# Six convolutions moved from GpSimd to TensorE, and the first sequence's helpers moved earlier, in a fused two-layer block

## Chip, cores and metric

The kernel runs on one core of a Trainium2 chip. Everything is one launch. The metric is the device time of that launch in microseconds (us); lower is better. The kernel before took 853.75 us in the median of three runs (847.93 to 856.35).

A core has five engines that each work through a list of instructions in order: TensorE (PE in the profile; its weight loads are listed apart as PEld), VectorE (DVE), ScalarE (ACT), GpSimd (POOL) and SyncE (SP), which here only issues transfers. An instruction that waits holds up all that stand behind it on its engine.

## What is computed

Two layers on an input of 4 sequences, 256 steps and 512 features, in float32. Layer 0 is attention plus a gated feed-forward; the change doesn't touch it. Layer 1 is a selective scan (Mamba) plus a small mixture of experts. This is the scan's part, shortened:

```python
proj = hidden_states @ in_proj_w                 # 512 -> 2 * 1024
x, z = jnp.split(proj, 2, axis=-1)               # each (4, 256, 1024), then transposed
xc = conv_b[None, :, None]
for k in range(4):                               # causal convolution along time, per channel
    xc = xc + conv_w[None, :, k:k + 1] * xp[:, :, k:k + Lq]
xc = jax.nn.silu(xc)
ssm_p = jnp.einsum('bdl,ed->ble', xc, x_proj_w)  # -> dt_r (32), Bm (16), Cm (16), each normalised
dt = jax.nn.softplus(jnp.einsum('blr,dr->bdl', dt_r, dt_proj_w) + dt_bias[None, :, None])
# per channel and state n = 0..15:  h_t = exp(dt_t * A_n) * h_(t-1) + dt_t * Bm_t * x_t ;  y_t = sum_n Cm_t * h_t
y = (ys + D_param[None, :, None] * xc) * jax.nn.silu(z)
return jnp.einsum('bdl,hd->blh', y, out_proj_w)
```

## The kernel before

**Tiling.** The 1024 channels of layer 1 are 8 chunks of 128 (`DC`), and two chunks are a pair, so that a sequence has four pairs. The 16 states are four groups (`NU`). One scan handles one chunk and one group for all 256 steps: 128 rows by 4 x 256 values. A sequence is 32 scans (`PER`), the four sequences are 128. Below, "scan u" is scan u of the sequence named, counted from 0, and "pair (b, p)" is pair p of sequence b.

**One scan's chain.** `decays` (ACT, L958, four instructions) makes exp(dt A). `scan_in` (DVE, L964) makes bx in PSUM from two spread inputs: `brow` and `dus`. `scan` (DVE, L979) runs the recurrence into tile `h`, and GpSimd multiplies it by C into tile `hc` (L984). `states_sum` (PE, L996) sums `hc` into the PSUM tile `ysum`, of which there is one. After a chunk's four scans `close_chunk` (DVE, L1000) multiplies `ysum` by the silu of z, `sz`; the next chunk's first sum (L994) waits for that.

**Order.** It is written out by hand. The main loop runs over the scans; for scan u it records, in this order: `decays(u + 2)`; the side work listed for u with `put`; `scan_in(u)`; a `close_chunk` if scan u - 2 was the last of its chunk; `scan(u)`; the side work listed with `put_late`; and `states_sum(u - 1)`. Each engine gets its instructions in that order.

**The side work that the change touches.**

- *Convolution* of the next sequence, two chunks at a time. `px_mm` (PE, L753) fills the PSUM tile `px`. `conv_in` (ACT) copies it into a padded tile (L762), makes four diagonal matrices `dg` for the first chunk (L767), and for the second chunk writes one product with the bias (L768) and three products `tap` (L772). `conv_taps` multiplies the four diagonals with shifted views of the padded tile on PE (L789, four matmuls), lets ACT add the bias (L791), and adds the second chunk's three taps on GpSimd (L795). Sequence 0's own convolution, before the loop, is done otherwise and stays.
- *Step widths* of the second half of sequence 0: `step_in` (PE and ACT, scans 5 and 6), `step_exp` (ACT, scan 7), `step_out` (three GpSimd additions L892, L894, L896 for each of two quarters q, the last followed by a store `dtd` to DRAM), `step_x` (GpSimd product L903 and store `dud`), and `spread`, which reads a chunk back into `dts` or `dus` with four transfers. All these transfers stand in one list on SP, together with the loads of weights `w_in`, `bw`, `lb` and `ow`.
- *The end of layer 0.* The last matmuls `po` of layer 0 (`down`, L469) run beside scans 0 to 2. Their memory becomes the pool `act` (`open_act`), which holds most tiles `h`, `hc` and two of three `decay` tiles. Because that memory is taken until then, scans 0 to 3 use lent tiles: the table `lent` names, per scan, a tag of another tile that is free for a while (`w_in`, `u`, `e`, `lw`). `step_in` writes the next tile with the tag `u`, `step_exp` those with `e` and `lw`. A new tile under a tag waits for the last reader of the old one.
- `add_last` (DVE, L481) adds the last row blocks of layer 0 after scans 1, 3 and 4; the one after scan 4 needs the very last `po`.

The order before, for the lines that the change edits:

```python
for q, us in enumerate(((5, 6, 7), (10, 12, 14)) if b else ((8, 9, 11), (15, 17, 18))):
    for k in range(3):
        put(b, us[k], step_out, b, 1, q, k)
for p, u in ((2, 8 if b else 13), (3, 16 if b else 19)):
    put(b, u, step_x, b, p)
for c in range(2, DC):
    o = 0 if b or c < 4 else 2
    put(b, 3 if c == 2 and not b else 4 * c - 6 + o, spread, "dt", b, c)
    put(b, 4 * c - 4 + o, spread, "du", b, c)
```

The pairs of sequence b + 1 are convolved beside sequence b: `conv_in` of pair p at scan 9 + 2p of sequence 0 and 8 + 2p of the others, `conv_taps` one scan later.

Of the kernel before, what the change touches and what calls it, by code (L numbers as in the profile page):

```python
# [8 lines left out]
F32 = mybir.dt.float32  # L9

F32R = mybir.dt.float32r
AF = mybir.ActivationFunctionType
ALU = mybir.AluOpType
# [4 lines left out]
P = 128  # L18
B, S, D = 4, 256, 512
# [6 lines left out]
DIN, NST, KC, RK = 1024, 16, 4, 32  # L26
# [11 lines left out]
V_CW, V_CB, V_DB, V_AL, V_D, V_END = 0, 4, 5, 6, 22, 23  # L38
# [3 lines left out]
def block_kernel(  # L42
# [24 lines left out]
    nc = tc.nc  # L67
    mm = nc.tensor.matmul
# [50 lines left out]
    live = {}  # L119
# [530 lines left out]
    NU = NST // NG  # L650
# [97 lines left out]
    def px_mm(b, p, i):  # L748
# [3 lines left out]
        for hc in range(HC):  # L752
            mm(px[:, i, :], lhsT=w[:, i, hc, :], rhs=xns[b][:, hc, :],  # L753
               start=(hc == 0), stop=(hc == HC - 1))

    def conv_in(b, p):


        px = live["px", b, p]
        if p == 0:  # L760
            xcs[b] = (act if b % 3 else w1).tile([P, DC, S], F32, tag=f"xc{b % 3}", name="xc")
        nc.scalar.copy(pads[p % 2][:, :, KC - 1 :], px)  # L762
        v = [vec[:, 2 * p + i, :] for i in range(2)]
        if b:
            dg = live["dg"] = w1.tile([P, KC, P], F32, tag="dg", name="dg")
            for k in range(KC):
                nc.scalar.activation(dg[:, k, :], ident, AF.Identity, scale=v[0][:, V_CW + k : V_CW + k + 1])  # L767
        nc.scalar.activation(xcs[b][:, 2 * p + 1, :], px[:, 1, :], AF.Identity,  # L768
                             bias=v[1][:, V_CB : V_CB + 1], scale=v[1][:, V_CW + KC - 1 : V_CW + KC])
        tp = w1.tile([P, KC - 1, S], F32, tag="tap", name="tap")  # L770
        for k in range(KC - 1):
            nc.scalar.activation(tp[:, k, :], pads[p % 2][:, 1, k : k + S], AF.Identity,  # L772
                                 scale=v[1][:, V_CW + k : V_CW + k + 1])
        live["tap"] = tp
        if b == 0:
            nc.scalar.activation(px[:, 0, :], px[:, 0, :], AF.Identity, bias=v[0][:, V_CB : V_CB + 1],
                                 scale=v[0][:, V_CW + KC - 1 : V_CW + KC])

    def conv_taps(b, p):
        px, c = live["px", b, p], 2 * p  # L780
        if b == 0:
            for k in range(KC - 1):
                nc.vector.scalar_tensor_tensor(
                    px[:, 0, :] if k < KC - 2 else xcs[b][:, c, :], pads[p % 2][:, 0, k : k + S],
                    vec[:, c, V_CW + k : V_CW + k + 1], px[:, 0, :], ALU.mult, ALU.add,
                )
        else:
            for k in range(KC):
                mm(px[:, 0, :], lhsT=live["dg"][:, k, :], rhs=pads[p % 2][:, 0, k : k + S],  # L789
                   start=(k == 0), stop=(k == KC - 1))  # L790
            nc.scalar.activation(xcs[b][:, c, :], px[:, 0, :], AF.Identity,  # L791
                                 bias=vec[:, c, V_CB : V_CB + 1])
        xc = xcs[b][:, c + 1, :]
        for k in range(KC - 1):
            nc.gpsimd.tensor_tensor(xc, xc, live["tap"][:, k, :], ALU.add)  # L795

    def conv_silu(b, z=None):
        nc.scalar.activation(xcs[b], xcs[b], AF.Silu)
# [130 lines left out]
    def gate_silu(b, *ps):  # L929
# [5 lines left out]


    lent = {
        "d": ("d", "w_in", "d", "w_in"), "h": ("w_in", "u", "e", "u"),
        "hc": ("w_in", "lw", "w_in", "lw"),
    }  # L940

    def lend(n, u):
# [56 lines left out]
    def close_chunk(b, c):  # L999
        nc.vector.tensor_tensor(  # L1000
            xcs[b][:, c, :], ysum, szs[b, c // 2][:, c % 2, :], ALU.mult
        )
# [216 lines left out]
    for b in range(B):  # L1219
# [36 lines left out]
        put(b, 2 if b else 6, step_in, b, 1, 1)  # L1256
        put(b, 3 if b else 7, step_exp, b, 1)

        for q, us in enumerate(((5, 6, 7), (10, 12, 14)) if b else ((8, 9, 11), (15, 17, 18))):
            for k in range(3):  # L1260
                put(b, us[k], step_out, b, 1, q, k)
        for p, u in ((2, 8 if b else 13), (3, 16 if b else 19)):
            put(b, u, step_x, b, p)
        for c in range(2, DC):
            o = 0 if b or c < 4 else 2
            put(b, 3 if c == 2 and not b else 4 * c - 6 + o, spread, "dt", b, c)
            put(b, 4 * c - 4 + o, spread, "du", b, c)
        put(b, 10, load_z, b, 2)
# [64 lines left out]
    for u in range(total + 2):  # L1333
        if 3 <= u < total - 2:
            decays(u + 2)
        for f, a in at.get(u, ()):
            f(*a)
        if u < total:
            if u:
                scan_in(u)  # L1340
        last = u - 2
        if last >= 0 and last % NU == NU - 1:
            c = last % PER // NU
            close_chunk(last // PER, c)
            if last // PER == B - 1:
                late.append(c)
        if u < total:
            scan(u, 1 if u < total - 1 else 4)
            if u < 3:
                decays(u + 2)  # L1350
        for f, a in late_at.get(u, ()):
            f(*a)
        if late and u >= total - PER + 22:
            c = late.pop(0)
            for i in range(2):
                out_mm(B - 1, i, c)
        if 1 <= u <= total:
            states_sum(u - 1)
        if u < 3:
            go(ff, (9, 12, 100)[u])  # L1360
        if u == 2:
            open_act()
# [105 lines left out]
```

## Time and profile before

The profile is of one execution, which took 852.26 us; its span on the core is 850.5 us, so 1.8 us lie around it. The median of the three runs is 853.75 us.

| engine | busy us | share of the span | what it does most |
|---|---|---|---|
| TensorE | 740.6 | 87% | matmuls of both layers |
| VectorE | 669.6 | 79% | scans L979 (288.0), inputs L964 (157.7) |
| ScalarE | 538.6 | 63% | decays L958 (213.3) |
| GpSimd | 489.1 | 58% | products L984 (301.6), taps L795 (32.8) |

The first scan's input starts at 333 us and the last scan ends at about 839 us, so the scan loop is 506 us of the span. Durations that recur below: a scan input takes 1.23 us and a scan 2.29 us, and where VectorE waits for nothing two scans are 3.69 us apart; the product on GpSimd takes 2.36 us; three taps on GpSimd take 2.34 us; the four matmuls of a diagonal convolution take 2.00 us, with the next work starting 1.84 us after their start. In time lines a row is: start in us, duration in us, engine, line, operation, output and inputs with their shapes, how many were merged, and in brackets the idle time of the engine just before it with what ended it. PEclk is the TensorE clock that was granted, as a share of the full one.

### The profile page before, as it was taken

To read this page: it belongs to the slowest core of one execution; us is meant where nothing else is said; L and a number is where in the kernel's file an instruction comes from. 1 tells how busy PE (TensorE), PEld (TensorE's weight loads), DVE (VectorE), ACT (ScalarE), POOL (GpSimd) and SP (SyncE) were. 2 spreads that over 40 slices of the span, in tenths; PEclk is the share of its full clock that TensorE was granted. 3 is DMA by queue.
4 is the path that set the end of the run, shared out by engine and by line. 5 is a ranking of instruction groups with operands and counts; after the bars stand their busy time and mean duration, and the time that the engine had idled before them with its cause. 6 is when DMAs were issued, how large, how long until landed. Compare 5 with 4: busy or idle time off the path is not lost.

```text
span 850.5 us, 10982 instructions
## 1 busy us (share of the span) xinstructions
PE 740.6 (87%) x3798; PEld 423.6 (50%) x3798; DVE 669.6 (79%) x647; ACT 538.6 (63%) x1061; POOL 489.1 (58%) x376
## 2 busy tenths in 40 slices
PE   5999999989999899989778888887898997956875
PEld 3565546656555676656444346344356444312331
DVE  4597755478744435798799999899999999999996
ACT  4225565223566267599885789786888885855561
POOL 3223322001343333669967689869599759697664
PEclk9999999899999999999898999989999979998998
DMA  7234332001222322555751644433553343443400
GB/s 223 68 94 125 88 86 62 0 1 38 75 75 79 113 56 63 139 147 161 206 142 50 173 137 124 123 100 109 156 155 99 102 112 102 109 119 105 112 25 25
DMA packets 67202, 86.71 MB, mean 102 GB/s; under 512 B 12061, under 2 KB 52009, under 8 KB 66762
## 3 DMA queue, kind: packets, MB, share of 16 engines
q1 hardware_dynamic: 57786, 67.12, 28.5%
q0 software_dynamic: 9072, 18.35, 7.8%
q8 instruction: 30, 0.49, 0.2%
q10 hardware_dynamic: 288, 0.52, 0.2%
q14 instruction: 26, 0.21, 0.1%
HBM read 66.58 MB, written 10.22 MB: 90 GB/s over the span
## 4 chain that ended last, share of the span: by engine, by line
PE 37%; DVE 30%; POOL 12%; ACT 8%; issue 6%; DMA 4%; SPq 1%; DVEq 0%; POOLq 0%; ACTq 0%
DVE h L979 18%; POOL hc L984 7%; PE pu L444 6%; PE pg L444 6%; DVE bx L964 6%; ACT decay L958 4%; PE av L397 4%; PE po L469 3%; PE scT L386 2%; DVE mpl L354 2%; PE px L753 2%; POOL xc L795 2%; PE pz L926 2%; DMA dus<-dud 2%; PE ysum L996 1%
## 5 line engine op out<-in xcount | busy, mean ns | idle before, releaser
L984 POOL TENSOR_TENSOR hc<-h,cr 128x1024 f32<-128x1024 f32 (+1 forms) x130 | 301.6, 2322 | 96.4 <-DVE h L979 76.6
L979 DVE TENSOR_TENSOR_SCAN h<-decay,bx 128x1024 f32<-128x1024 f32 (+1 forms) x129 | 288.0, 2234 | 16.3 <-PE po L469 4.0
L958 ACT ACTIVATE decay<-dts,aneg 128x255 f32<-128x255 f32 x504 | 213.3, 498 | 97.5 <-DVE h L979 87.2
L964 DVE TENSOR_TENSOR bx<-brow,dus 128x1024 f32<-128x1024 f32 x128 | 157.7, 1232 | 8.7 <-DMA dus<-dud 4.6
L996 PE MATMUL ysum<-hc,stack 128*32 128x256 f32 x1024 | 88.1, 413 | 60.1 <-POOL hc L984 59.8
L456 POOL TENSOR_TENSOR hlo<-g,hhi 128x512 fp32r<-128x512 f32 x28 | 35.9, 1281 | 118.3 <-ACT hhi L455 118.3
L427 POOL DMA_DIRECT2D wgu<-in_wgu x56 | 31.2, 558 | 97.3 <-PE pg L444 95.9
L354 DVE TENSOR_REDUCE mpl<-sc 128x4 f32<-128x1024 f32 x64 | 76.4, 1217 | 12.4 <-PE sc L352 12.2
L996 PEld LDWEIGHTS ysum<-hc,stack 128*32 128x32 f32 x1024 | 21.2, 111 | 120.7 <-POOL hc L984 98.1
L388 ACT ACTIVATE pe<-scT 128x1024 f32<-128x1024 f32 x64 | 64.0, 1023 | 23.4 <-PE sc L352 16.8
L1088 PE MATMUL po<-ow,xc 128*128 128x512 f32 x128 | 70.4, 659 | 2.2 <-DVE xc L1000 2.2
L926 PE MATMUL pz<-xn1T,w_in 128*128 128x256 f32 x256 | 67.5, 411 | 0.0
L753 PE MATMUL px<-xn1T,w_in 128*128 128x256 f32 x256 | 61.8, 387 | 0.1
L926 PEld LDWEIGHTS pz<-xn1T,w_in 128*128 128x128 f32 x256 | 49.0, 200 | 19.0 <-issue 10.8
L753 PEld LDWEIGHTS px<-xn1T,w_in 128*128 128x128 f32 x256 | 48.2, 192 | 13.1 <-issue 4.3
L452 DVE SCALAR_TENSOR_TENSOR g<-g,pg 128x512 f32<-128x512 f32 x28 | 19.2, 686 | 41.5 <-ACT g L451 41.5
L444 PE MATMUL pu<-xhi,wgu 128*128 128x512 f32 x112 | 48.7, 435 | 2.3 <-DMA wgu<-in_wgu 2.3
L469 PE MATMUL po<-wd,hhi 128*128 128x512 f32 x112 | 50.3, 449 | 0.0
L444 PE MATMUL pg<-xhi,wgu 128*128 128x512 f32 x112 | 48.9, 437 | 0.0
L455 ACT CAST hhi<-g 128x512 fp32r<-128x512 f32 x28 | 17.3, 619 | 48.5 <-DVE g L454 48.5
L444 PE MATMUL pu<-xlo,wgu 128*128 128x512 f32 x112 | 45.4, 405 | 0.0
L469 PE MATMUL po<-wd,hlo 128*128 128x512 f32 x112 | 45.0, 401 | 0.0
(230 smaller groups left out, 1251.7 us busy)
## 6 DMA issues: line engine op xcount, KB each, us to landing
dts<-dtd SPq DMA_DIRECT2D x124, 128.0 KB, 2.9
dus<-dud SPq DMA_DIRECT2D x124, 128.0 KB, 3.0
wgu<-in_wgu POOLq DMA_DIRECT2D x56, 256.0 KB, 2.8
w_in<-in_inx SPq DMA_DIRECT2D x16, 512.0 KB, 4.3
w_in<-in_inz SPq DMA_DIRECT2D x16, 512.0 KB, 4.9
dtd<-dt SPq DMA_DIRECT2D x15, 256.0 KB, 2.2
dud<-du SPq DMA_DIRECT2D x15, 256.0 KB, 2.2
wd<-in_wd POOLq DMA_DIRECT2D x7, 512.0 KB, 3.6
```

The costliest lines, as they stand in the source:

```text
L354: nc.vector.tensor_reduce(mpl2[b % 2][:, qb, 2 * hp : 2 * hp + 2, 16 + 2 * gq : 18 + 2 * gq], sc.rearrange("p i (f k) -> p i f k", f=2), A ...
L388: nc.scalar.activation(pes[b, k][:, 2 * t : 2 * t + 2, :], sc, AF.Exp)
L444: mm(ps, lhsT=wgus[i][:, hc, :], rhs=xs[j][:, hc, :], start=(hc == 0 and j == 0), stop=(hc == HC - 1 and j == 1))
L469: mm(po, lhsT=hids[th][j][:, m, i * P : (i + 1) * P], rhs=wd[:, m, :], start=False, stop=(m == MC - 1 and j == 1))
L753: mm(px[:, i, :], lhsT=w[:, i, hc, :], rhs=xns[b][:, hc, :], start=(hc == 0), stop=(hc == HC - 1))
L926: mm(pz[:, i, :], lhsT=w[:, i, hc, :], rhs=xns[b][:, hc, :], start=(hc == 0), stop=(hc == HC - 1))
L958: nc.scalar.activation(da[:, k, 1:], live["dts", b, c][:, k, 1:], AF.Exp, scale=aneg[:, c, k, g : g + 1])
L964: nc.vector.tensor_tensor(bx, brow[g // 2][:, g % 2, :].unsqueeze(1).to_broadcast([P, NG, S]), live["dus", b, c], ALU.mult)
L979: nc.vector.tensor_tensor_scan(h[:, n].rearrange("p n t -> p (n t)"), da[:, n].rearrange("p n t -> p (n t)"), bx[:, n].rearrange("p n t -> ...
L984: (nc.vector if k == NG - 1 else nc.gpsimd).tensor_tensor(hc[:, n], h[:, n], crows[b][:, g, :].unsqueeze(1).to_broadcast([P, NG // parts, ...
L996: mm(ysum[k * NB : (k + 1) * NB, :], lhsT=stack, rhs=hc[:, k, :], start=False, stop=(g == NU - 1))
L1088: mm(live["po", b, i], lhsT=xcs[b][:, c, i * P : (i + 1) * P], rhs=late_w["ow"][:, c, :], start=False, stop=(c == DC - 1))
```

## The change

Three things change; all lie in layer 1's loop.

1. For six pairs, (1, 0), (1, 3), (2, 1), (2, 3), (3, 1) and (3, 3), the second chunk is convolved as the first is: ACT makes four more diagonals in the memory of `tap`, PE multiplies them into the second half of `px`, and ACT adds the bias. The three GpSimd additions, the biased product L768 and the three taps L772 go, for these pairs.
2. In sequence 0 `step_out`, `step_x` and the spreads of chunks 4 to 7 stand one or two scans earlier.
3. Scan 4 of sequence 0 gets lent tiles too (`h` in `e`, `hc` in `u`), and the first `close_chunk` moves from before scan 5 to behind it.

```diff
+    both = ((1, 0), (1, 3), (2, 1), (2, 3), (3, 1), (3, 3))
+
     def conv_in(b, p):
...
-        nc.scalar.activation(xcs[b][:, 2 * p + 1, :], px[:, 1, :], AF.Identity,
-                             bias=v[1][:, V_CB : V_CB + 1], scale=v[1][:, V_CW + KC - 1 : V_CW + KC])
-        tp = w1.tile([P, KC - 1, S], F32, tag="tap", name="tap")
-        for k in range(KC - 1):
-            nc.scalar.activation(tp[:, k, :], pads[p % 2][:, 1, k : k + S], AF.Identity,
-                                 scale=v[1][:, V_CW + k : V_CW + k + 1])
-        live["tap"] = tp
+        tp = live["tap"] = w1.tile([P, KC - 1, S], F32, tag="tap", name="tap")
+        if (b, p) in both:
+            tp = tp.rearrange("p k t -> p (k t)")
+            for k in range(KC):
+                nc.scalar.activation(tp[:, k * P : (k + 1) * P], ident, AF.Identity,
+                                     scale=v[1][:, V_CW + k : V_CW + k + 1])
+        else:
...
     def conv_taps(b, p):
...
         xc = xcs[b][:, c + 1, :]
-        for k in range(KC - 1):
-            nc.gpsimd.tensor_tensor(xc, xc, live["tap"][:, k, :], ALU.add)
+        if (b, p) in both:
+            dg = live["tap"].rearrange("p k t -> p (k t)")
+            for k in range(KC):
+                mm(px[:, 1, :], lhsT=dg[:, k * P : (k + 1) * P], rhs=pads[p % 2][:, 1, k : k + S],
+                   start=(k == 0), stop=(k == KC - 1))
+            nc.scalar.activation(xc, px[:, 1, :], AF.Identity, bias=vec[:, c + 1, V_CB : V_CB + 1])
+        else:
+            for k in range(KC - 1):
+                nc.gpsimd.tensor_tensor(xc, xc, live["tap"][:, k, :], ALU.add)
...
     lent = {
-        "d": ("d", "w_in", "d", "w_in"), "h": ("w_in", "u", "e", "u"),
-        "hc": ("w_in", "lw", "w_in", "lw"),
+        "d": ("d", "w_in", "d", "w_in"), "h": ("w_in", "u", "e", "u", "e"),
+        "hc": ("w_in", "lw", "w_in", "lw", "u"),
     }
...
-        for q, us in enumerate(((5, 6, 7), (10, 12, 14)) if b else ((8, 9, 11), (15, 17, 18))):
+        for q, us in enumerate(((5, 6, 7), (10, 12, 14)) if b else ((8, 9, 10), (13, 15, 16))):
...
-        for p, u in ((2, 8 if b else 13), (3, 16 if b else 19)):
+        for p, u in ((2, 8 if b else 11), (3, 16 if b else 17)):
             put(b, u, step_x, b, p)
         for c in range(2, DC):
-            o = 0 if b or c < 4 else 2
+            o = 0 if b or c < 4 else 1
...
-            close_chunk(last // PER, c)
+            if c or last > NU:
+                close_chunk(last // PER, c)
...
             scan(u, 1 if u < total - 1 else 4)
+            if last == NU - 1:
+
+                close_chunk(0, 0)
```

On the engines this gives: PE has four more matmuls (and ACT one more biased copy) right behind the diagonal convolution of each of the six pairs; GpSimd lacks 18 additions; on SP the store `dtd` of chunks 4 and 5 comes before the loads `w_in` and `bw`, the store `dud` before a spread and the loads `w_in` and `lb`, and the later stores and spreads of sequence 0 follow one or two places earlier.

## The prediction

> **What bounds the kernel now.** The page first: TensorE is busiest, yet the chain that ended last is shared.
>
> ```profile
> PE 740.6 (87%) x3798; PEld 423.6 (50%) x3798; DVE 669.6 (79%) x647; ACT 538.6 (63%) x1061; POOL 489.1 (58%) x376
> PE 37%; DVE 30%; POOL 12%; ACT 8%; issue 6%; DMA 4%; SPq 1%; DVEq 0%; POOLq 0%; ACTq 0%
> ```
>
> Layer 0 gives TensorE's share; the scan loop, 333 to 839 us, is the stage to read. So next VectorE's instructions in order of time, keeping those with idle time in front. These are all of 0.3 us or more up to the last scan:
>
> ```profile
> 355.55 2.29 DVE L979 TENSOR_TENSOR_SCAN h<-decay,bx 128x1024 f32<-128x1024 f32 x1 [3.96 <-PE po L469]
> 360.74 0.43 DVE L1000 TENSOR_TENSOR xc<-ysum,sz 128x256 f32<-128x256 f32 x1 [1.18 <-ACT sz L932]
> 376.83 0.42 DVE L1000 TENSOR_TENSOR xc<-ysum,sz 128x256 f32<-128x256 f32 x1 [1.17 <-PE ysum L996]
> 394.64 0.43 DVE L1000 TENSOR_TENSOR xc<-ysum,sz 128x256 f32<-128x256 f32 x1 [2.87 <-PE ysum L996]
> 407.78 1.23 DVE L964 TENSOR_TENSOR bx<-brow,dus 128x1024 f32<-128x1024 f32 x1 [3.18 <-DMA dus<-dud]
> 424.03 1.23 DVE L964 TENSOR_TENSOR bx<-brow,dus 128x1024 f32<-128x1024 f32 x1 [1.43 <-DMA dus<-dud]
> 541.28 0.42 DVE L1000 TENSOR_TENSOR xc<-ysum,sz 128x256 f32<-128x256 f32 x1 [1.82 <-PE ysum L996]
> 571.84 0.42 DVE L1000 TENSOR_TENSOR xc<-ysum,sz 128x256 f32<-128x256 f32 x1 [0.53 <-PE ysum L996]
> 664.02 0.42 DVE L1000 TENSOR_TENSOR xc<-ysum,sz 128x256 f32<-128x256 f32 x1 [1.39 <-PE ysum L996]
> ```
>
> They sum to 17.5 us, 13.8 of it in sequence 0. That is all a change to helpers can win here: the loop is VectorE's, 3.69 us a scan, and the question is only what becomes of these waits. Sequence 0 needs the other engines' lists. ACT, then PE:
>
> ```profile
> 365.04 0.45 ACT L853 ACTIVATE u<-pdt,vec 128x256 f32<-128x256 f32 x1
> 382.86 1.70 ACT L958 ACTIVATE decay<-dts,aneg 128x255 f32<-128x255 f32 x4
> 384.69 0.47 ACT L791 ACTIVATE xc<-px,vec 128x256 f32<-128x256 f32 x1
> 365.64 0.66 PE L996 MATMUL ysum<-hc,stack 128*32 128x256 f32 x8
> 366.63 1.13 PE L848 MATMUL pdt<-nrm,dtw 32*128 32x256 f32 x4 [0.32 <-ACT dt L854]
> 381.81 2.84 PE L789 MATMUL px<-pad,dg 128*128 128x256 f32 x8 [2.05 <-ACT xc L768]
> 384.45 2.77 PE L753 MATMUL px<-xn1T,w_in 128*128 128x256 f32 x8
> 390.21 2.00 PE L789 MATMUL px<-pad,dg 128*128 128x256 f32 x8
> ```
>
> ACT is busy without a gap from 355.50 to 384.56, and again from 387.26 to 409.8; PE idles only 0.32, 2.05 and 0.33 us from 365 to 410. So there VectorE has slack, and PE and ACT have none. One more view, stretches with the granted clock (third number from the right):
>
> ```profile
> 381.80:384.50 2.70, 2.69 (x9) 2.21 (x10) 2.56 (x2) 2.70 (x7) 2.54 (x4) 0.69 0.00 0
> 387.20:390.00 2.80, 2.80 (x25) 1.70 (x24) 2.67 (x2) 2.74 (x8) 2.80 (x3) 1.00 0.52 127
> ```
>
> After 2.05 us of idle PE ran at 0.69 for 5.4 us.
>
> **Scan 4 in lent tiles.** Its decay is ready at 347.8 and its input bx at 351.6, so it runs 351.6 to 353.9 instead of from 355.55. But `add_last` behind it needs the last `po`, 355.5. Then 0.66 for it, 1.23 for bx 5, and scan 5 at 357.4 (its decay, ACT from 355.50, is ready at 357.15). `close_chunk` still has to await `sz`, 360.11 + 0.60. It ends at 361.1, and scan 6 starts at 362.4, not 364.73: 2.3 us early.
>
> **What the lent `u` costs.** `step_in` of scan 5 writes the next `u`, so its first ACT instruction (365.04) now waits for the sums of scan 4, recorded after it on PE: 365.64 + 0.66, so 366.37, 1.33 later. PE can't be earlier: its transposes before wait for ACT's xnt (1.92 us idle to 362.89), and xnt follows `sz`. Queued behind on ACT are the rest of `step_in`, two copies, the decays of scan 8 and `step_exp`; on PE pdt L848 waits for the buffer that ACT empties, 366.63 becoming 367.96, and from there PE runs back to back to the sums of scan 7. So the second `close_chunk` moves from 376.83 to 378.16. At scan 9 the 2.3 us early are 1.3 us late. (At nothing, if PE were ahead; a wait can't gain.)
>
> **Pair (1, 0), two groups on PE.** ACT: four diagonals (1.18 us) and a second biased copy (0.40) replace the product (0.45) and the taps (1.20): equal. PE: 1.84 us more. The built order adds a turn: the second group writes the same `px` tile and waits for ACT's copy L791 of the first, and ACT has the decays of scan 12 ahead of that copy. With the shift of 1.33 the copy runs 385.4 to 385.85. The first group may start with its first diagonal, 381.8, and ends at 383.7, so PE stands 2.2 us. No row shows this turn; bounds from the rows: 0.5 us (ACT's 0.47 copy alone) and 2.2. I take 2.2, since ACT's list here has no gap. Then the second group and px L753 take either 1.84 + 1.83 (390.21 to 392.05 and on, full clock) or 2.64 + 2.70 (381.81 to 387.15). The sums of scan 9 so start at 389.6 or 391.2, against 387.15: 2.45 or 4.05 late. The nearest row, 2.05 us idle, had the slow clock, and so had 1.92 and 2.24: I take 4.05. The Trainium skill, "TensorE: Matmul & The Clock Gate", Part 1, says the clock halves after at least one idle window of some 3.4 us; the trace disagrees (0.69 after 2.05), and with the rule the full-clock end of my sum would hold.
>
> PE and ACT carry this on without a gap: the copy for pair (1, 1) waits for px. The third `close_chunk` comes at 397.1 or 398.6, not 394.64.
>
> **Step widths earlier.** GpSimd loses the taps of (1, 0); L896 follows the product of scan 9 and ends near 385.2 instead of 388.45. `dtd` goes out before `w_in` and `bw` instead of behind them, where it took 6.66 us. `dud` now stands behind both (the `w_in` waits for px, 389.6 to 391.2), so give it those 6.7 us: landed by 399, spread by 404. VectorE wants it 9.66 us after scan 13 begins (394.98 to 404.64 before), that is 407.1 or 408.6. The 3.18 us go, but scan 16 starts at most 0.7 earlier or 0.8 later: the lateness of PE has eaten them. The first spread of chunk 5 comes behind `dud` of the next quarter on SP, that is behind L903 of scan 17, ending at 416.5 or so; landed by 422, when VectorE asks at 425 or later. So 1.43 us go.
>
> **Pair (1, 3).** Again 1.84 us and a turn, now behind the decays of scan 18. The sums of scan 15, ended at 410.0 before, end at 415.1 (full) or 417.5 (slow). The fourth `close_chunk`, at 412.61 before, waits for them: 2.5 or 5.0 late. Less 1.43, sequence 0 costs 1.1 or 3.6 us.
>
> **Sequences 1 and 2.** GpSimd was last there: from 497 to 540 it has no gap, and taps of 2.3 us sit ahead of its products.
>
> ```profile
> 535.44 2.33 POOL L795 TENSOR_TENSOR xc<-xc,tap 128x256 f32<-128x256 f32 x3
> 537.73 2.35 POOL L984 TENSOR_TENSOR hc<-h,cr 128x1024 f32<-128x1024 f32 x1
> ```
>
> Without them the product of scan 15 ends at 536.9, not 540.1. PE takes its place: group one of (2, 1) 516.21 to 518.05, turn 0.7, group two to 520.6, then px, sums (0.57), px, and the sums of scan 11 start at 524.85, not 523.80: a new wait of 1.0 at `close_chunk`. On the same list px L753, L994, sums, pz (1.84), sums, pz, two groups with a turn of 0.5, sums, out (1.0), sums: `close_chunk` at 540.95, not 541.28. So -0.3. In sequence 2 the router's 1.05 us (pr L1011) stand on that list too: 123.15 us later that gives 665.15 against 664.02, +1.1. The turns are short there because ACT has gaps; PE has none over 0.8 us, so the clock stays up.
>
> **Sum.** 852.26 (span 850.5 plus 1.8 around it) + 3.6 - 0.3 + 1.1 = 856.7. With full clock 854.2. The execution lies 1.5 us under the median of the runs, inside their spread of 8.4; I leave that in the range.
>
> **Rivals.** *The waits simply go.* Removed 3.96, 3.18, 1.43, 1.82, 1.39 = 11.8: 840.5; if PE keeps half of it, 846. For it: in sequence 0 the chain runs through GpSimd's additions and the two stores, in sequence 1 through GpSimd at 33%. Against: the waits of 1.17 and 2.87 between them are PE's. *No net effect* (853 to 854): the turn in (1, 0) takes 0.5, or the clock stays full. *The turn takes PE down everywhere* (slower): if ACT's copy lies behind the decays in the four later pairs as in (1, 0), each pays 1.5 us more and 0.8 + 0.87 for the slow clock, 4 x 3.2 = 12.7 on top, 869; decisive once PE stands 1.9 us or more there. *The earlier steps do nothing* lies inside the forecast: their 4.6 us are covered by PE either way.
>
> **Chances.** Forecast 0.55 (852 to 861), no net effect 0.18, waits go 0.15, turn everywhere 0.12. About 1% is what a measurement of this kernel can tell from no change: faster means under 845.2, a half of the third case, 0.08; slower means over 862.3, the last case and an edge of the first, 0.14; else 0.78. The range 847 to 863 leaves out the lower half of the third case and nearly all of the last.
>
> **What would show it.** Right: scan 4 of sequence 0 without wait for po; ACT's `u` L853 (new line) waiting for ysum; PE idle some 2 us between two groups of (1, 0) under a clock below 0.8; no wait for dus at scans 16 and 20, instead some 4 us for ysum at the fourth `close_chunk`; near 1 us for ysum at the third one of sequences 1 and 2. Wrong: PE's second group directly behind the first, or VectorE's waits in sequence 0 under 10 us in all.

## The result, and the profile after

The kernel after took 857.54 us in the median of 6 runs (856.82 to 861.11), the kernel before 853.81 (847.93 to 856.35, 6 runs beside them). The ratio is 1.0059, with a 95% interval of 1.0031 to 1.0087: a small loss, inside the 1% that was called no change. The medians lie 3.7 us apart; the forecast was 4.4. Single runs of one kernel are spread by as much as that: of 12 runs of a version below (no turn, router earlier) five took 850.3 to 850.8 us and seven 854.9 to 856.6. So a profile, which is of one run, needn't add up to a ratio. The profiled execution took 857.5 us with a span of 855.7, against 852.26 and 850.5.

First the page of the kernel after, busy time by engine and shares of the chain that ended last:

```profile
PE 751.1 (88%) x3846; PEld 431.4 (50%) x3846; DVE 671.3 (78%) x647; ACT 537.9 (63%) x1067; POOL 477.2 (56%) x358
PE 48%; DVE 24%; ACT 19%; issue 3%; POOL 3%; DMA 2%; SPq 0%; ACTq 0%; DVEq 0%; POOLq 0%
```

TensorE is 10.5 us busier, GpSimd 11.9 us less, and GpSimd's share of the chain fell from 12% to 3%. The work did move. Now VectorE's instructions in order of time in the kernel after: start, duration, and in brackets the idle time in front with what ended it. The scan is now L994, `close_chunk` L1015, and the first step of the router L1050 and L1051. The router chooses the experts, for two sequences at a time, beside sequences 0 and 2; its values `ml` are made by small matmuls on TensorE (`pr`) and copied by ACT.

```profile
353.49 0.69 DVE L481 TENSOR_TENSOR x<-x,po 128x512 f32<-128x512 f32 x1 [1.47 <-PE po L469]
368.92 2.29 DVE L994 TENSOR_TENSOR_SCAN h<-decay,bx 128x1024 f32<-128x1024 f32 x1 [1.27 <-ACT decay L973]
378.22 0.42 DVE L1015 TENSOR_TENSOR xc<-ysum,sz 128x256 f32<-128x256 f32 x1 [5.74 <-PE ysum L1011]
395.36 0.42 DVE L1015 TENSOR_TENSOR xc<-ysum,sz 128x256 f32<-128x256 f32 x1 [2.19 <-PE ysum L1011]
413.76 0.42 DVE L1015 TENSOR_TENSOR xc<-ysum,sz 128x256 f32<-128x256 f32 x1 [3.48 <-PE ysum L1011]
525.42 0.43 DVE L1015 TENSOR_TENSOR xc<-ysum,sz 128x256 f32<-128x256 f32 x1 [1.10 <-PE ysum L1011]
540.97 0.42 DVE L1015 TENSOR_TENSOR xc<-ysum,sz 128x256 f32<-128x256 f32 x1 [0.60 <-PE ysum L1011]
573.19 0.42 DVE L1015 TENSOR_TENSOR xc<-ysum,sz 128x256 f32<-128x256 f32 x1 [2.19 <-PE ysum L1011]
650.18 0.42 DVE L1015 TENSOR_TENSOR xc<-ysum,sz 128x256 f32<-128x256 f32 x1 [1.10 <-PE ysum L1011]
666.66 0.42 DVE L1015 TENSOR_TENSOR xc<-ysum,sz 128x256 f32<-128x256 f32 x1 [1.53 <-PE ysum L1011]
685.76 0.19 DVE L1050 TENSOR_REDUCE m<-ml 128x4 f32<-128x32 f32 x1 [1.13 <-ACT ml L1028]
```

The waits for `dus` (3.18 and 1.43) and most of the one for `po` are gone, as meant. In their place VectorE waits for TensorE: 5.74 at the second `close_chunk`, 2.19 at the third, 3.48 at the fourth. In sequences 1 and 2 the third `close_chunk` has a new wait of 1.10, and two more places are late: 573.19, where the kernel before waited 0.53, and 685.76, where it did not wait.

To compare executions, I take the start of each scan less the start of scan 0 of sequence 0. That is needed because the loop begins anywhere from 329.4 to 337.0 us in the 14 profiles of this study, although layer 0 is the same code in all of them. The table has the time from the loop's start to scan 9 of sequence 0 (behind the second `close_chunk`), the lengths of three sequences, and the ratio of the runs. In sequence 3 the last scan started 115.0 to 115.1 us after the first in all profiles but two (115.5).

| kernel | scan 9 | seq. 0 | seq. 1 | seq. 2 | ratio to before | 95% interval |
|---|---|---|---|---|---|---|
| before | 42.8 | 142.1 | 123.2 | 125.6 | 1 | |
| after | 46.2 | 143.9 | 124.8 | 129.1 | 1.0059 | 1.0031 to 1.0087 |
| second part alone | 46.5 | 144.1 | 123.1 | 125.5 | 0.9994 | 0.9964 to 1.0024 |
| first part alone | 42.9 | 143.7 | 123.1 | 129.1 | 1.0085 | 1.0052 to 1.0119 |
| third part alone | 44.8 | 143.4 | 122.2 | 125.5 | 1.0002 | 0.9973 to 1.0031 |
| after, `hc` in `lw` | 42.8 | 144.8 | 126.2 | 129.1 | 1.0083 | 1.0052 to 1.0115 |
| after, `route_exp` at 23 | 46.1 | 143.9 | 123.1 | 131.2 | 1.0125 | 1.0091 to 1.0159 |
| first part, (1, 0) (1, 3) | 43.0 | 144.9 | 124.3 | 125.5 | 1.0046 | 1.0023 to 1.0070 |
| first part, other four | 42.8 | 142.6 | 123.1 | 129.1 | 1.0067 | 1.0034 to 1.0099 |
| after, no turn | 46.1 | 141.5 | 121.7 | 127.8 | 1.0026 | 0.9999 to 1.0054 |
| no turn, router earlier | 46.1 | 141.6 | 121.8 | 126.5 | 1.0010 | 0.9983 to 1.0037 |
| the same, `lw`, PE kept busy | 42.8 | 139.2 | 123.5 | 128.2 | 0.9990 | 0.9970 to 1.0010 |
| second and third part, router earlier | 43.0 | 138.9 | 122.1 | 125.6 | 0.9970 | 0.9945 to 0.9996 |
| before, router earlier | 46.3 | 142.8 | 123.0 | 125.6 | 0.9989 | 0.9959 to 1.0018 |

### The profile page after: what moved, and what is told of

Same layout as the page of the kernel before. It is cut to its first block, busy times and chain, and to the rows that moved or that the text cites. A ratio compares the mean times of both kernels' runs of the same rounds, so it can differ in the third digit from the quotient of the medians.

```text
span 855.7 us, 11051 instructions
## 1 busy us (share of the span) xinstructions
PE 751.1 (88%) x3846; PEld 431.4 (50%) x3846; DVE 671.3 (78%) x647; ACT 537.9 (63%) x1067; POOL 477.2 (56%) x358
## 4 chain that ended last, share of the span: by engine, by line
PE 48%; DVE 24%; ACT 19%; issue 3%; POOL 3%; DMA 2%; SPq 0%; ACTq 0%; DVEq 0%; POOLq 0%
DVE h L994 14%; ACT decay L973 10%; PE pg L444 6%; PE pu L444 5%; PE po L469 5%; PE av L397 4%; DVE bx L979 3%; PE px L753 3%; PE ysum L1011 3%; POOL hc L999 2%; PE po L1103 2%; PE scT L386 2%; PE pz L941 2%; DVE mpl L354 2%; PE pp L824 2%
## 5 line engine op out<-in xcount | busy, mean ns | idle before, releaser
L994 DVE TENSOR_TENSOR_SCAN h<-decay,bx 128x1024 f32<-128x1024 f32 (+1 forms) x129 | 288.0, 2235 | 13.6 <-ACT decay L973 1.3
L941 PE MATMUL pz<-xn1T,w_in 128*128 128x256 f32 x256 | 69.6, 420 | 0.0
L941 PEld LDWEIGHTS pz<-xn1T,w_in 128*128 128x128 f32 x256 | 50.1, 205 | 19.7 <-issue 11.9
```

Of the source, the lines that this page charges most:

```text
L941: mm(pz[:, i, :], lhsT=w[:, i, hc, :], rhs=xns[b][:, hc, :], start=(hc == 0), stop=(hc == HC - 1))
L994: nc.vector.tensor_tensor_scan(h[:, n].rearrange("p n t -> p (n t)"), da[:, n].rearrange("p n t -> p (n t)"), bx[:, n].rearrange("p n t -> ...
```

## The experiments

**Each part alone, and the lent tile.** My first theory was that the loss comes from the lent `u` and from sequence 0, and that the earlier widths are a gain. Second part alone: before with the new scan numbers of `step_out`, `step_x` and `spread`.

> The kernel before, with sequence 0's step widths (step_out, step_x and the spreads of chunks 4 on) put one or two scans earlier, and nothing else. Theory (the loss of the change comes from the lent u in sequence 0 and from the second groups on TensorE; the earlier widths by themselves are a gain): the waits for dus of 3.18 us at scan 16 and 1.43 us at scan 20 go, and TensorE's own waits at close_chunk (1.17, 2.87) stay about as they were, so some 4 us less, a ratio to before of 0.994 to 0.997. Rival (TensorE's lateness takes back whatever VectorE gains there): the waits for dus go, but the ones for ysum at the third and fourth close_chunk grow by the same, 1.000, within 0.002.

Measured 0.9994 [0.9964, 1.0024]. The waits for `dus` fell from 3.18 and 1.43 to nothing and 0.36, but the second `close_chunk` waited 4.93 us instead of 1.17, and 2.25 us went at scan 22. This is nearer to the rival; the two losses come up again below.

First part alone:

> The kernel before, with the second chunk of the six pairs convolved by TensorE, and nothing else. Theory: the two pairs of sequence 0 put 1.84 us each and a turn on TensorE, whose sums the third and fourth close_chunk await; part of it hides in the waits for dus (3.18, 1.43), which stay. In sequences 1 and 2 GpSimd's wait is swapped for one of 1.1 us at the third close_chunk, and what follows costs some 1.5 us in each. 2 to 5 us more, a ratio of 1.002 to 1.006. Rival (the second groups are harmless, and all of the loss is the lent tiles'): sequence 0 as before, the products of GpSimd sooner, 0.998 to 1.000.

Measured 1.0085 [1.0052, 1.0119], above even the theory's range. By its median the first part alone is more than the whole loss, though its interval overlaps that of the kernel after. In the profile, which is of the fastest of its six runs, sequence 0 is 1.6 us longer and sequence 2 3.6 us.

Third part alone:

> The kernel before, with scan 4 of sequence 0 in lent tiles and the first close_chunk behind scan 5, and nothing else. Theory: the 2.3 us gained by scan 6 are lost to ACT's wait for the sums of scan 4 before it may write u; TensorE idles twice for 1.7 to 2 us, is granted 0.54 after it, and the second close_chunk waits some 5.7 us: scan 9 is 1.3 to 3.4 us late, the rest of sequence 0 carries it unless the wait for dus of 3.18 us covers it. Ratio 1.000 to 1.004. Rival (the lent u costs nothing that matters, and the gain at the front stays): 2.3 us less, 0.997.

Measured 1.0002 [0.9973, 1.0031]. TensorE idled as expected and the second `close_chunk` waited 5.51 us, so that scan 9 was 2.0 us late. The waits behind it covered that: the third `close_chunk`, 2.87 before, had none of 0.3 us or more, and the first wait for `dus` was 1.74 instead of 3.18. At scan 20 VectorE was 1.0 us ahead of the kernel before, and then lost 2.2 us at scan 22. By the ratio the third part costs nothing in the sum.

After, with the product of scan 4 in `lw`:

```diff
-        "hc": ("w_in", "lw", "w_in", "lw", "u"),
+        "hc": ("w_in", "lw", "w_in", "lw", "lw"),
```

> The kernel after, with the product of scan 4 put in the tile lw, where the product of scan 3 lay, and no longer in u. Theory (the lent u is what throws away the gain at the front): ACT's u no longer waits 1.56 us, TensorE's idle times ahead of the widths are short, its clock stays up over 361 to 372 us of the span, the second close_chunk waits 2 us or less, and scan 9 is 2 to 3.4 us sooner than in the kernel after; 2 to 3.5 us less than after, a ratio to before of 1.001 to 1.004. Rival (the widths wait for ACT's other work anyway, or the third close_chunk takes it back): as after, 1.004 to 1.008.

Here the theory fell as a statement on time. Two of its steps came true: ACT's wait was gone, and scan 9 lay at 42.8 instead of 46.2. Two did not: the second `close_chunk` still waited 3.49, and TensorE still idled 1.92 us ahead of the transposes and had a clock of 0.55, 0.50 and 0.81 from 361.8 to 366.3. The ratio was 1.0083 [1.0052, 1.0115], no better than after. In its profile the third `close_chunk` waited 3.92 us instead of 2.19, since TensorE, now on time at pair (1, 0), stood 2.00 us between the two groups instead of 1.22; and VectorE lost 2.27 us at scan 22 of sequence 0, where the kernel after lost nothing; in sequence 1 the sixth `close_chunk` waited 3.27 instead of 2.19.

**The router's subtraction.** Three kernels (the second part alone, the third part alone, and after with `hc` in `lw`) had lost the same 2.25 us or so at scan 22 of sequence 0, and all so far with the pairs (3, 1) and (3, 3) on TensorE lost 2.26 in sequence 2. The kernel after, VectorE then GpSimd in order of time:

```profile
685.76 0.19 DVE L1050 TENSOR_REDUCE m<-ml 128x4 f32<-128x32 f32 x1 [1.13 <-ACT ml L1028]
685.98 1.21 DVE L1051 TENSOR_TENSOR ex<-ml,m 128x32 f32<-128x32 f32 x1
687.11 1.22 DVE L979 TENSOR_TENSOR bx<-brow,dus 128x1024 f32<-128x1024 f32 x1
```

```profile
684.77 2.37 POOL L999 TENSOR_TENSOR hc<-h,cr 128x1024 f32<-128x1024 f32 x1 [1.92 <-DVE h L994]
```

A subtraction of 128x32 took 1.21 us and ended at 687.19; GpSimd's product ended at 687.14. The kernel before, same place:

```profile
681.86 0.16 DVE L1035 TENSOR_REDUCE m<-ml 128x4 f32<-128x32 f32 x1
682.06 0.19 DVE L1036 TENSOR_TENSOR ex<-ml,m 128x32 f32<-128x32 f32 x1
```

```profile
682.09 2.39 POOL L984 TENSOR_TENSOR hc<-h,cr 128x1024 f32<-128x1024 f32 x1 [1.89 <-PE ysum L996]
```

There it started 0.03 us ahead of the product and took 0.19. In the second part alone it started 0.31 us behind the product's start (430.17 against 429.86) and took 2.10, again to the product's end. Of the 28 such subtractions in the 14 profiles 20 took 0.19 us; 8 took 1.20 to 2.10, and each of the 8 ended 0.04 to 0.05 us after the product beside it. So the last `ml` has a due time: the end of scan 21. A copy a little late is paid for twice, by the wait and by the rest of the product.

What makes the copy late is TensorE's list, in part by way of ACT's. On ACT the copy stands behind four instructions of `step_in`, which wait for `pdt` on TensorE. ACT in the kernel before, then after:

```profile
679.97 0.47 ACT L853 ACTIVATE u<-pdt,vec 128x256 f32<-128x256 f32 x1 [0.53 <-PE pdt L848]
681.41 0.29 ACT L1013 COPY ml<-pr 128x136 f32<-128x136 f32 x1
```

```profile
683.99 0.47 ACT L868 ACTIVATE u<-pdt,vec 128x256 f32<-128x256 f32 x1 [0.81 <-PE pdt L863]
685.44 0.29 ACT L1028 COPY ml<-pr 128x136 f32<-128x136 f32 x1
```

In the kernel before the copy ended 0.25 us ahead of VectorE's scan 21 (681.70 against 681.95), in the kernel after 1.1 us behind it (685.73 against 684.63).

The first attempt to show it moved `route_exp` one scan later:

```diff
-                put(b, 22, route_exp, b)
+                put(b, 23, route_exp, b)
```

> The kernel after, with the first step of the router's choice (route_exp: a maximum and a subtraction on VectorE, an exponential on ACT) put at scan 23 of sequences 0 and 2 instead of 22. Theory (in sequence 2 TensorE's second groups make pr and so ACT's ml late; VectorE waits 1.13 us for it, and its 128x32 subtraction, L1051, then falls into GpSimd's product and lasts until that ends, 1.21 us instead of 0.19): both are gone, scan 22 of sequence 2 starts 2.26 us sooner than in the kernel after, and a subtraction that starts directly behind a scan takes 0.2 us. 2.3 us less than after, a ratio to before of 1.002 to 1.006, against some 1.007 for after. Rival (that lateness is PE's, and a later wait takes it): the subtraction is as slow at its new place, or the fourth close_chunk waits 2 us more, and the ratio stays at that of after, 1.005 to 1.009.

Measured 1.0125 [1.0091, 1.0159], worse than either expected. The subtraction did take 0.19 us and scan 22 was on time. But its reader moved too: VectorE in the changed kernel,

```profile
697.69 0.19 DVE L1042 TENSOR_REDUCE w<-ex 128x4 f32<-128x32 f32 x1 [4.46 <-ACT ex L1052]
```

and ACT:

```profile
696.96 0.57 ACT L853 COPY cr<-pcr 128x512 f32<-128x512 f32 x1
697.42 0.23 ACT L1052 ACTIVATE ex<-ex 128x32 f32<-128x32 f32 x1
```

The exponential L1052 now stood behind `step_exp` and a copy on ACT, and `route`, at scan 25 of sequence 2, waited 4.46 us for it. That makes sequence 2 2.1 us longer than in the kernel after. The ratio asks for more than 5 us, but the profile is of the fastest of the six runs (857.01 us, the median is 862.62); what the others lost beyond it isn't shown.

**Which pairs, and the turn.** The first part in two halves:

> The kernel before, with the second chunk convolved by TensorE in the pairs (1, 0) and (1, 3) alone, those that run beside sequence 0. The kernel with all six pairs had a ratio of 1.0085 [1.0052, 1.0119]; its profile has sequence 0 1.6 us longer and sequence 2 3.6 us longer than before. Theory (each stage pays for itself): sequence 0 some 1.6 us longer, sequences 1 and 2 as before; 1.002 to 1.004. Rival (all of the 1.0085 arises in sequence 0, where TensorE has no slack and the slow clock follows its idle times): 1.006 to 1.010.

> The kernel before, with the second chunk convolved by TensorE in the pairs (2, 1), (2, 3), (3, 1) and (3, 3) alone, those that run beside sequences 1 and 2. Theory: sequence 1 as long as before (1.15 us lost at the third close_chunk, 1.2 won at the fourth), sequence 2 3.5 us longer (1.13 at the third close_chunk, 2.26 at the router's subtraction of scan 22): a ratio of 1.004 to 1.005. Rival (the loss is sequence 0's): 0.998 to 1.001.

Measured 1.0046 [1.0023, 1.0070] and 1.0067 [1.0034, 1.0099]. The second rival falls; the first half lies above the theory's range and short of the rival's. The second half lies above the theory's range too, and both intervals reach into it. Sequences 0 and 2 each pay their own share. With (1, 0) and (1, 3) sequence 0 is 2.8 us longer in its profile, sequence 1 is 1.1 (a wait of 2.09 at the sixth `close_chunk`, though no second group runs beside it here), and sequence 2 is as before. With the other four sequence 2 is 3.5 us longer, 1.1 of it at the third `close_chunk` and 2.3 at the router, and sequence 1 as before.

Then the turn, which is TensorE's idle time between the two groups of a pair: in the kernel after both groups are put first, both of ACT's copies behind them (shortened; pairs with one group keep the old order).

```diff
             for k in range(KC):
                 mm(px[:, 0, :], ...)
-            nc.scalar.activation(xcs[b][:, c, :], px[:, 0, :], ...)
...
             for k in range(KC):
                 mm(px[:, 1, :], ...)
+            nc.scalar.activation(xcs[b][:, c, :], px[:, 0, :], ...)
             nc.scalar.activation(xc, px[:, 1, :], ...)
```

> The kernel after, with both groups of a pair put on TensorE one behind the other and ACT's two biased copies behind them, so that the second group does not wait for ACT's copy of the first. Theory (the turn is a real part of the loss): TensorE's idle time between the groups, 1.22 and 0.83 us in sequence 0 and 0.56 to 0.60 in the four other pairs, is gone; the third close_chunk of sequences 1 and 2 waits some 0.5 us instead of 1.10, and the third and fourth one of sequence 0 about 1 us less; 2 to 3 us less in all, a ratio of 1.003 to 1.005. Rival (the 1.84 us of matmuls alone set it, since TensorE then waits at its next instruction for ACT anyway): as after, 1.005 to 1.009.

Measured 1.0026 [0.9999, 1.0054]. The interval meets that of after, so the ratios alone don't part them; the profiles do. TensorE at pair (1, 0), after and then without the turn (in the second kernel the groups are L797 and L806):

```profile
381.00 2.00 PE L797 MATMUL px<-pad,dg 128*128 128x256 f32 x8
384.22 1.99 PE L805 MATMUL px<-pad,tap 128*128 128x256 f32 x8 [1.22 <-ACT xc L799]
```

```profile
379.32 2.00 PE L797 MATMUL px<-pad,dg 128*128 128x256 f32 x8
381.15 1.89 PE L806 MATMUL px<-pad,tap 128*128 128x256 f32 x8
```

and VectorE without the turn, at the third `close_chunk` of sequences 1 and 2:

```profile
520.59 0.42 DVE L1018 TENSOR_TENSOR xc<-ysum,sz 128x256 f32<-128x256 f32 x1 [0.22 <-PE ysum L1014]
...
642.34 0.42 DVE L1018 TENSOR_TENSOR xc<-ysum,sz 128x256 f32<-128x256 f32 x1 [0.23 <-PE ysum L1014]
```

The wait of 1.10 is 0.22, and the fourth wait of sequence 0 is 2.59 instead of 3.48. The router's loss in sequence 2 stayed (1.13 of wait, and a subtraction of 1.20). So the turn is a real part of the loss. Of the 3.0 us by which sequence 1 is shorter than in the kernel after, though, 1.4 are the sixth `close_chunk`'s (0.79 instead of 2.19), which is a matter of the clock and not of the turn (last section).

**Versions with the router earlier.** The router's matmuls go forward and `route_exp` stays:

```diff
-                for i, u in enumerate((16, 19, 20, 21)):
+                for i, u in enumerate((16, 17, 19, 20)):
                     put(b, u, router, b, i)
```

> The kernel after with the two groups of a pair back to back on TensorE and ACT's two copies behind them (as in the kernel whose ratio was 1.0026 [0.9999, 1.0054]), and the router's matmuls of sequences 0 and 2 put at scans 16, 17, 19 and 20 instead of 16, 19, 20 and 21; route_exp stays at scan 22. Theory (TensorE's lateness makes ml late, and VectorE pays for it twice, by a wait of 1.13 us and by a subtraction that lasts until GpSimd's product ends): the last ml is there before scan 21 ends, the subtraction takes 0.2 us, scan 22 of sequence 2 starts 2.26 us sooner; a ratio of 0.998 to 1.000. Rival (the router's matmuls, put earlier, make the sums of scans 17 to 20 late and a later wait takes it back): 1.002 to 1.004.

Measured 1.0010 [0.9983, 1.0037], between the two. The subtraction took 0.19 us in both sequences, but of 2.26 us sequence 2 kept only 1.3: the fifth `close_chunk` waited 1.35 us for TensorE instead of 0.42.

Next the lend to `lw`, and matmuls that keep TensorE busy where it idled:

```diff
         pt = psmm.tile([P, HC, P], F32, tag="mm", name="pt")
+        if (b, i) == (1, 0):
+            for k in range(8):
+                mm(pt[:, k % HC, :], lhsT=ident, rhs=ident, start=True, stop=True)
```

> As the kernel with groups back to back and the router earlier, with two edits more: the product of scan 4 in lw and not in u, and eight matmuls of 128x128, whose results are overwritten, ahead of the transposes of sequence 1's first block (L737), where TensorE idled 1.92 us in every profile. Theory (second close_chunk: the wait of 1.2 to 5.7 us that differs from execution to execution is made by the slow clock that follows TensorE's idle time at scans 5 and 6): no stretch between scans 5 and 9 of sequence 0 has a clock under 0.9, the second close_chunk waits 2 us or less instead of 5.7, 2 to 4 us less than the kernel without the two edits, a ratio of 0.994 to 0.997. Rival (ACT's list sets it, and the third close_chunk takes the rest): 0.998 to 1.001.

Measured 0.9990 [0.9970, 1.0010], in the rival's range. The clock part held: it was 1.00 throughout from scan 5 to past scan 9. These are stretches of the kernel with the second part alone, which has the idle time, and of this one. Columns: stretch, length, busy time of PE, PEld, DVE, ACT and POOL, granted clock, DMA share, GB/s.

```profile
361.20:363.00 1.80, 1.75 (x10) 1.11 (x10) 1.70 (x2) 1.80 (x5) 1.25 (x1) 0.93 0.00 0
363.00:366.00 3.00, 2.19 (x12) 1.08 (x12) 2.93 (x2) 3.00 (x9) 1.71 (x2) 0.50 0.43 132
366.00:369.00 3.00, 3.00 (x14) 1.36 (x13) 2.87 (x2) 3.00 (x9) 1.76 (x1) 0.50 0.91 264
369.00:372.00 3.00, 3.00 (x11) 1.85 (x13) 2.83 (x3) 2.97 (x6) 2.35 (x1) 0.50 1.00 210
372.00:375.00 3.00, 3.00 (x18) 2.10 (x11) 1.93 (x2) 2.94 (x4) 1.24 (x2) 0.84 0.03 11
```

```profile
358.60:361.60 3.00, 2.95 (x23) 2.55 (x23) 2.90 (x3) 2.99 (x5) 3.00 (x2) 1.00 0.33 130
361.60:364.60 3.00, 1.63 (x15) 0.81 (x14) 2.83 (x3) 3.00 (x9) 2.98 (x2) 1.00 0.20 61
364.60:367.60 3.00, 3.00 (x19) 2.02 (x19) 2.83 (x3) 3.00 (x9) 1.67 (x2) 1.00 0.86 217
```

But the wait at the second `close_chunk` was 3.50, not 2 or less. Scan 9 lies at 42.8, exactly where the kernel before has it. In both kernels the second `pdt` on TensorE, which waits for ACT's `dt`, starts 32.26 and 32.25 us after the loop's start (at 366.63 in the kernel before, a row of the prediction, and here at 364.37), and from there TensorE has no gap up to the sums:

```profile
364.37 1.12 PE L869 MATMUL pdt<-nrm,dtw 32*128 32x256 f32 x4 [1.37 <-ACT dt L875]
```

So ACT's list sets this floor, as the rival had it, and the 2.3 us won ahead of scan 6 can't pass it (1.17 + 2.33 = 3.50). The kernel after with `hc` in `lw` is at the floor too, with half the clock for 3.4 us ahead of `pdt`; against that profile the extra matmuls won nothing here. What other profiles have above the floor, 2.0 to 3.7 us, goes with the lent `u` or with a slow clock past the start of `pdt`; two kernels that don't lend `u` show 3.5 and 3.7, and in them the clock was 0.50 for 10.2 us in one piece.

Sequence 0 did become 2.4 us shorter than without the two edits, but sequences 1 and 2 became 1.7 longer each: the sixth `close_chunk` of sequence 1 waited 1.93 instead of 0.78, and in sequence 2 the fifth waited 1.71 instead of 1.35, behind a wait of 1.22 for ACT. Ahead of both places the clock fell to 0.50 for 3.4 us (from some 539 and 662 us) where it stayed at 1.00 without the edits; whether that made the waits isn't shown.

Last, the second and third part without the first, and the control:

> The kernel before with the change's second and third part, the product of scan 4 in lw and not in u, and the router at scans 16, 17, 19 and 20; all second chunks stay with GpSimd. The parts alone gave 0.9994 [0.9964, 1.0024] and 1.0002 [0.9973, 1.0031], and in both profiles VectorE was ahead of the kernel before at scan 20 (0.3 and 1.0 us) and then lost 2.25 us at the router's subtraction of scan 22. Theory (both parts are a gain that the router takes back): no loss at scan 22, waits for dus under 0.5 us, 2 to 5 us less than before, a ratio of 0.994 to 0.998. Rival (TensorE's lateness takes it at the second to fourth close_chunk, whatever the router does): 0.999 to 1.002.

> The kernel before with the router's matmuls of sequences 0 and 2 at scans 16, 17, 19 and 20, and nothing else: the control for the kernel that had this edit along with the second and third part and a ratio of 0.997 [0.9945, 0.9996]. Theory (the two parts make VectorE early, and the router then takes it back; before them VectorE is late enough that its last ml is there): in the profile of before the subtraction took 0.19 us already, so the edit alone has nothing to win; sequence 0 between 141.5 and 143 us, a ratio of 0.999 to 1.001. Rival (the router's edit is the whole gain, the parts give nothing): 0.995 to 0.998.

The first measured 0.9970 [0.9945, 0.9996], 847.74 us against 852.1: the fastest of all kernels here. Its VectorE from scan 5 to scan 19 of sequence 0:

```profile
358.45 0.42 DVE L1000 TENSOR_TENSOR xc<-ysum,sz 128x256 f32<-128x256 f32 x1 [1.00 <-ACT sz L932]
374.72 0.42 DVE L1000 TENSOR_TENSOR xc<-ysum,sz 128x256 f32<-128x256 f32 x1 [3.68 <-PE ysum L996]
386.31 2.29 DVE L979 TENSOR_TENSOR_SCAN h<-decay,bx 128x1024 f32<-128x1024 f32 x1 [0.33 <-POOL hc L984]
391.33 0.42 DVE L1000 TENSOR_TENSOR xc<-ysum,sz 128x256 f32<-128x256 f32 x1 [1.47 <-PE ysum L996]
407.07 0.43 DVE L1000 TENSOR_TENSOR xc<-ysum,sz 128x256 f32<-128x256 f32 x1 [0.79 <-PE ysum L996]
412.04 2.29 DVE L979 TENSOR_TENSOR_SCAN h<-decay,bx 128x1024 f32<-128x1024 f32 x1 [1.08 <-POOL hc L984]
418.51 1.23 DVE L964 TENSOR_TENSOR bx<-brow,dus 128x1024 f32<-128x1024 f32 x1 [0.49 <-DMA dus<-dud]
```

No wait is over 3.7, `dus` costs 0.49, and sequence 0 is 3.2 us shorter than before, all of it there by scan 20 (87.8 against 91.0) and kept at scan 22. The control gave 0.9989 [0.9959, 1.0018]: the router's edit alone is no gain that can be seen, and its subtraction took 0.19 us as it had before. The two intervals overlap, though. That the two parts gain what the router took from each of them is what the profiles show (a loss at scan 22 in each part alone, none here); the ratios alone don't settle it. Nor is the gain split: this kernel also has the product of scan 4 in `lw`, which neither part alone had.

## Why the prediction was right, and where it was not

The time, 857.54 against a forecast of 856.7, was right, and so was its main reason: VectorE's waits for transfers give way to waits for TensorE, which has no slack in sequence 0. That the sum came so near is in part luck. By sequence the forecast was +3.6, -0.3 and +1.1; the profile of the kernel after shows +1.8, +1.6 and +3.6.

- **Scan 4.** "2.3 us early" at scan 6: 2.33 measured. "At scan 9 the 2.3 us early are 1.3 us late": 3.4. ACT did wait for the sums before `u` (1.56 us, forecast 1.33). What was left out is the clock. These are ACT's wait, TensorE's rows, and two stretches with the clock (third number from the right):

```profile
364.71 0.47 ACT L868 ACTIVATE u<-pdt,vec 128x256 f32<-128x256 f32 x1 [1.56 <-PE ysum L1011]
```

```profile
360.89 1.82 PE L737 MATMUL pt<-cst,xnt 128*128 128x128 f32 x8 [1.94 <-ACT xnt L729]
366.33 1.13 PE L863 MATMUL pdt<-nrm,dtw 32*128 32x256 f32 x4 [1.75 <-ACT dt L869]
367.95 3.68 PE L753 MATMUL px<-xn1T,w_in 128*128 128x256 f32 x8
```

```profile
361.00:364.00 3.00, 3.00 (x18) 1.79 (x18) 2.93 (x2) 2.14 (x5) 1.22 (x1) 0.54 0.00 0
367.90:371.60 3.70, 3.70 (x16) 2.48 (x14) 2.64 (x2) 3.70 (x11) 0.92 (x1) 0.54 1.02 235
```

TensorE idled 1.94 us ahead of its transposes and 1.75 ahead of pdt, and ran at 0.54 behind each. Pdt started 1.7 us late (33.95 after the loop's start against 32.26), and px took 3.68 us instead of 1.99, 1.7 more. In the third part alone the clock was still full at the first place, and pdt was only 0.4 late (32.63). I had given the slow clock to the second groups only.
- **Pair (1, 0).** "I take 4.05" is the step that failed: the third `close_chunk` came 2.7 us late (less than the 3.4 at scan 9), and the step's error is the clock, which was 1.00 from 380 to 384 and on to the next sums. The turn was 1.22 for a forecast "2.2 us", but only because TensorE itself came late to the pair; in the three profiles where it came on time (the first part alone, its half with (1, 0) and (1, 3), and after with `hc` in `lw`) the turn was 2.00, and even behind that the clock stayed at 1.00. Nor did "0.69 for 5.4 us" in the kernel before mean 5.4 us of slow clock: a mean of 0.69 over 5.4 us is 3.4 us at 0.50, which costs 1.7. With the pairs (1, 0) and (1, 3) alone, scan 13 is 1.0 us later than before. My low end, 2.45 less the 1.33 carried in, had it. I took the other because the row with the nearest idle time, 2.05, had the slow clock.
- **Step widths.** "The 3.18 us go" and "1.43 us go" both held, and "the lateness of PE has eaten them" too, as long as the first part is in.
- **Pair (1, 3).** "2.5 or 5.0 late" at the fourth `close_chunk`: 3.1 late, with a wait of 3.48 and a turn of 0.83. Less the 1.43 that went, sequence 0 is +1.8 for +3.6 in all.
- **Sequence 1.** "-0.3" was right up to the fourth `close_chunk` (1.10 and 0.60 of wait, so -0.1). The rest of the +1.6 is the wait of 2.19 at the sixth: TensorE idled 1.66 us ahead of 562.5, as it did in the kernel before, and in both the clock then fell to 0.50; but it stayed there for 10.2 us in the kernel after and for 6.8 in the kernel before (from means over stretches of 1 us). The first part alone had 6.8 and waited 0.55, so the long wait needn't come with it. Whether the first part makes it likelier stays open: 1.9 to 3.3 us in 4 of the 9 profiles that have some of it (in one of the four not beside sequence 1), under 0.8 in the 5 that have none.
- **Sequence 2.** "+1.1" was right for the two `close_chunk` (1.10 and 1.53). The step that failed is where I stopped: I followed TensorE's list to the sums and no further, though the same list holds the `pdt` and the router's matmuls that ACT's copy `ml` stands behind, and that copy is due at the end of scan 21. That cost 2.26 us more.
- **The base.** Layer 0 was 2.0 us shorter in the profiled execution of after than in that of before. The loop was 6.9 us longer where I forecast 4.4, and the span 5.2.

Of the signs named ahead, PE idle "some 2 us" under "a clock below 0.8" at pair (1, 0) did not come; the others did, with 3.48 for "some 4 us" at the fourth `close_chunk`.

Of the rivals, "no net effect" had the right clock at (1, 0) but a cheaper sum than was true. "The turn takes PE down everywhere" was wrong: at the four later pairs the turns were 0.56 to 0.60, and the clock around them was 1.00. "The waits simply go" failed as written, since TensorE was next; only without the first part did some of them go.

The long subtraction agrees with the Trainium skill, "SBUF — State Buffer", section "SBUF: two separate sides", which says that a VectorE operation on two tensors with both inputs in SBUF contends with GpSimd's reads, and that the second to start is held up for the whole instruction. The eight that ended with the product are what that would look like. So are the router's later steps on 128x32, which have an input in PSUM: some 120 of them started inside a product in the 14 profiles, and all took 0.19 or 0.20 us (in the kernel before L1029 at 443.45, 0.42 us behind the product's start). No run here changed the place of an input to test the port itself.

## What to carry to other kernels

Before moving work to another engine, list everything that stands behind it on that engine's list with a due time, the small and rare instructions too, and not only the sums that the next big step awaits. An edit that makes the leading engine earlier gains only up to the next due time that someone else sets; move that first, with its readers on every queue, or a good edit measures as nothing. When two parts write one tile in turn, issue both before anything reads it.

## What the hardware did that I had not expected

- After the same idle time of 1.92 us on TensorE, at the same place in the program, the clock of 0.50 lasted some 3.4 us in the kernel before (reckoned from 0.88, 0.50 and 0.76 in three stretches of 2 us from 360.8) and 10.2 us in the kernel with the second part alone (from 0.93, three times 0.50 and 0.84 above), though the two don't differ on TensorE up to there. In the third part alone the clock was still 1.00 until 361.9, 4.0 us after that idle time had ended. The second `close_chunk` of kernels with an unchanged front waited 1.17 to 1.36 us in four profiles, all with 3.4 us of slow clock there, and 4.65 to 4.93 in two, both with 10.2. One profile is one draw of this. The lengths come in steps: between scans 5 and 9 of sequence 0 the 14 profiles show pieces of 3.4 or 10.2 us (none in the kernel with the extra matmuls), and behind the 1.66 us of idle time on TensorE ahead of `pcr` in sequence 1 (562.50 in the kernel after) the clock was at 0.50 for 3.4 us in two profiles, 6.8 in nine and 10.2 in three. Nor does the idle time alone say whether the clock falls: it fell around the 2.05 us at pair (1, 0) in the kernel before and not around the turns of 2.00 at the same pair. The Trainium skill, "TensorE: Matmul & The Clock Gate", Part 1, says that the window over which activity is judged runs free of the program; the spread would fit that, but no run here shows the window itself.
- A start 0.03 us ahead of GpSimd's product or 0.3 us behind it made the same VectorE subtraction of 128x32 last 0.19 or 2.10 us.
